# First-layer scores from one product of both mixing weights with x, in a two-layer f32 kernel

## The chip, the cores and the metric

The kernel runs on one core of a Trainium2 chip. The metric is the device time of one execution in microseconds (us). Three timed runs of the kernel before gave 1794.26, 1794.6 and 1798.48 us, a median of 1794.6. One more execution was profiled; its durations are the ones that the text uses.

The engines are called by their short names: PE is TensorE (PEld its weight loads), DVE is VectorE, ACT is ScalarE, POOL is GpSimd, SP is the engine that issues most DMAs.

## What is computed

Two layers over 32 batches. The first is a cross-attention of 128 channels by 512 positions per batch, the second a recurrent block (RWKV) that takes four batches as one group. Only the first layer matters here:

```python
def _L0_xattn_ref(x_c, x_s, Wn, bn, Wm, bm, Wl, bl, Wo, bo):
    Mn = _conv1x1(Wn, bn, _inorm(x_c))          # [128, 512] per batch
    Mm = _conv1x1(Wm, bm, _inorm(x_s))
    A = jax.nn.softmax(jnp.einsum('bct,bcs->bts', Mn, Mm), axis=-1)   # 512 x 512 per batch
    Ml = _conv1x1(Wl, bl, x_s)
    Mo = jnp.einsum('bcs,bts->bct', Ml, A)
    return _conv1x1(Wo, bo, Mo) + x_c
```

`_inorm` takes mean and variance of each channel over the 512 positions; `_conv1x1(W, b, x)` is W times x plus a bias per output channel. With x and y for the two normalised inputs, the score of token t against position s is

(Wn x_t + bn) . (Wm y_s + bm) = (Wm' Wn x_t + Wm' bn) . y_s + (Wn' bm . x_t + bn . bm),

where ' is the transpose. The last bracket does not depend on s: it is the same for all scores of token t. All arithmetic is f32.

## The kernel before

Everything that the engines execute in the main part is first recorded and then ordered. A call such as `K.tensor.matmul(...)` does not issue an instruction; it appends an operation with an estimated duration to a list (`Program.record`, `cost`). A list scheduler (`schedule`, `order_of`) simulates the five engines, gives out the buffers (8 PSUM banks, 44 work tiles of 128x512, 40 small tiles, 4 weight tiles of 1 MB) and fixes one order per engine; `pace` moves some DMAs. The rank of an operation is its place in the program, moved by the length of its chain and by a number of the table `SHIFTS` for its stage; the names with "+" apply to the last groups as well. `with K.bunch(ns)` makes several instructions one operation of the given duration. Since every recorded instruction is issued from the same helper, nearly all of them carry line 246 in the profile, and groups are told apart by tiles: `bank` is a PSUM bank, `t` a work tile, `small` a small tile, `wring` a big weight.

The first layer, `layer0(b)`, handles one batch: it loads x_c and x_s (256 KB each), takes statistics on DVE (`bn_stats`, `bn_aggr`), the reciprocal root on POOL, and normalises both inputs on DVE. Each normalised input goes through one product with its own 128x128 weight into a PSUM bank, from which ACT adds the bias: m_n and m_m. A third small set of products makes the values (four products of 128 columns with `wol`, the product of Wl and Wo). Then, for each of the four blocks `tb` of 128 tokens: one product of 128x512 scores, the negated maximum of each token's scores on DVE, exp on ACT with that maximum as bias and the sum as a second output, reciprocal and scaling on DVE. Sixteen transposes through PE and four products with the values finish the batch.

The first layer of a group is not run by itself. `ahead(place)` inserts the next group's batches into the second layer of the current one, and the scheduler uses them to fill PE while the recurrence works on DVE. Set-up stands outside the recorded part: the loads of four 128x128 weights and the biases on ACT's queue, and two products, `wol` and `bol` (lines 661 and 665).

In f32 each product is executed as two passes, so one matmul statement gives two matmul records and two weight loads.

Of the kernel before, what the change touches and what calls it, by code (L numbers as in the profile page):

```python
# [12 lines left out]
F32 = mybir.dt.float32  # L13
AF = mybir.ActivationFunctionType
ALU = mybir.AluOpType
# [3 lines left out]
P = 128  # L19
# [7 lines left out]
NC = E // P  # L27
# [33 lines left out]
SWITCH = 95  # L61
ROUNDS, TRACE, BLAME = 16, 20000, 0.001
SHIFTS = {
    "first0": -306, "first0+": -95, "first1": 2, "first1+": -122, "first2": -40,
    "first2+": -7, "first3": 24, "first3+": 203, "front": 7, "front+": 157, "gates": -67,
    "gates+": -1, "head": -121, "head+": 51, "levels0": -68, "levels0+": -71, "levels2": 20,
    "levels2+": -152, "mixes": 81, "mixes+": -41, "norm": 78, "norm+": -310,
    "outputs0": -277, "outputs0+": 238, "outputs2": -235, "outputs2+": -661,
    "recurrence0": -14, "recurrence0+": -48, "recurrence2+": -68, "rows": 85, "rows+": 306,
    "squares": -88, "squares+": 77, "values0": -56, "values0+": -63, "values2": 33,  # L70
    "values2+": 81,
}
REACH, PULL = 200, 0.003
WORDS, REFILL = 280, 3200
# [534 lines left out]
def xattn_then_rwkv(ctx: ExitStack, tc: tile.TileContext, a: dict, out: bass.AP):  # L609
    nc = tc.nc  # L610

    const = ctx.enter_context(tc.tile_pool(name="const", bufs=1))
    psum = ctx.enter_context(tc.tile_pool(name="psum", bufs=1, space=PSUM))

    def slots(tag, count, shape, space=const):
        return [space.tile(shape, F32, tag=f"{tag}{i}", name=f"{tag}{i}") for i in range(count)]

    banks = Pool(slots("bank", 8, [P, 512], psum))
# [10 lines left out]
    K = Program(nc, tc)  # L629

    def bank():
        return View(Tensor(banks, [P, 512]))

    def wt(shape=(P, 512)):
        return View(Tensor(work, list(shape)))
# [4 lines left out]
    def st_(*shape):  # L640
        return View(Tensor(small, [P, *shape]))


    ident = const.tile([P, P], F32, tag="ident", name="ident")
# [5 lines left out]
    w0 = {}  # L650
# [5 lines left out]
    bias = {n: bias4[:, i : i + 1] for i, n in enumerate(BIASES)}  # L656


    wol = const.tile([P, P], F32, tag="wol", name="wol")
    p0 = banks.tiles[7]  # L660
    nc.tensor.matmul(p0[:, 0:P], w0["Wl0"], w0["WoT0"], start=True, stop=True)
# [103 lines left out]
    def mean_rstd(stats, n):  # L765

        mv, rstd = st_(n, 2), st_(n)
        for i in range(n):
            K.vector.bn_aggr(mv[:, i, :], stats[:, i, :])
        K.vector.tensor_scalar(rstd, mv[:, :, 1], EPS, None, ALU.add)  # L770
        K.gpsimd.tensor_tensor(rstd, rstd, neg_half[:, 0:n], ALU.pow)
        return mv, rstd
# [10 lines left out]
    def layer0(b):  # L783
        K.stage = ("first", b, str(b % G))
        x_c, x_s = wt(), wt()
        K.held = begun.get(b - 2)
        K.sync.dma_start(x_c, a["x"][b])
        K.held = begun.get(b - 2)
        K.sync.dma_start(x_s, a["ctx_2048"][b])
        stats = st_(2, 6)  # L790
        K.vector.bn_stats(stats[:, 0, :], x_c)
        K.vector.bn_stats(stats[:, 1, :], x_s)
        mv, rstd = mean_rstd(stats, 2)
        m = []
        for i, (src, w, bi) in enumerate(((x_c, "WnT", "bn"), (x_s, "WmT", "bm"))):
            xn = wt()
            K.vector.tensor_scalar(
                xn, src, mv[:, i, 0:1], rstd[:, i : i + 1], ALU.subtract, ALU.mult
            )
            pm = bank()  # L800
            K.tensor.matmul(pm, w0[w], xn, start=True, stop=True)
            t = wt()
            K.scalar.activation(t, pm, AF.Identity, bias=bias[bi])
            m.append(t)
        m_n, m_m = m


        pv = bank()
        for sb in range(NC):
            K.tensor.matmul(  # L810
                pv[:, sb * P : (sb + 1) * P], x_s[:, sb * P : (sb + 1) * P], wol,
                start=True, stop=True,
            )
        vals = wt()
        K.scalar.copy(vals, pv)


        e = []
        for tb in range(NC):
            sc = bank()  # L820
            if tb == 0:
                begun[b] = K.ops[-1]
            K.tensor.matmul(sc, m_n[:, tb * P : (tb + 1) * P], m_m, start=True, stop=True)
            nmax, den = st_(1), st_(1)
            K.vector.tensor_reduce(nmax, sc, AX.X, ALU.max, negate=True)
            t = wt()
            K.scalar.activation(t, sc, AF.Exp, bias=nmax, accum_out=den)
            K.vector.reciprocal(den, den)
            K.vector.tensor_scalar(t, t, den, None, ALU.mult)
            e.append(t)  # L830
        po = bank()
        for sb in range(NC):
            pt = bank()
            for tb in range(NC):
                K.tensor.transpose(
                    pt[:, tb * P : (tb + 1) * P], e[tb][:, sb * P : (sb + 1) * P], ident
                )
            at = wt()
            K.scalar.copy(at, pt)
            K.tensor.matmul(  # L840
                po, vals[:, sb * P : (sb + 1) * P], at, start=(sb == 0), stop=(sb == NC - 1)
            )
        K.vector.scalar_tensor_tensor(x_c, po, bol, x_c, ALU.add, ALU.add)
        return x_c
# [256 lines left out]
    def layer1(g, xs):  # L1101
        following = []

        def ahead(place):

            stage = K.stage
            if g + 1 < NG:
                for i in (AHEAD if g + 2 < NG else AHEAD_LAST)[place]:
                    following.append(layer0((g + 1) * G + i))
            K.stage = stage  # L1110
# [190 lines left out]
    def feed_forward(g, xs, ws):  # L1301
# [42 lines left out]
        yield  # L1344

    xs = [layer0(0), layer0(1)]
    constants()
    xs += [layer0(2), layer0(3)]
    for g in range(NG):
        xs = layer1(g, xs)  # L1350
# [42 lines left out]
```

## Time and profile before

| | us |
|---|---|
| median of three runs | 1794.6 |
| profiled execution | 1798.06 |
| its span, first to last instruction | 1796.3 |
| PE busy | 1758.5 (98%) |
| PE weight loads busy | 888.7 (49%) |
| DVE busy | 1171.4 (65%) |
| ACT busy | 706.2 (39%) |
| POOL busy | 310.3 (17%) |
| PE, products of a normalised input with its weight (WnT and WmT, 128 records) | 67.5 |
| ACT, bias of these products (64 records) | 43.3 |

A group line of the profile reads: line, engine, operation, out<-in, array tile or shape, count, then busy time and mean duration in ns of one, then the idle time of the engine before them and what ended it. Matmul records overlap: a record of a 512-column pass has a mean of some 600 ns, though in a stream the passes follow each other at 429 ns. A timeline line gives the start in us, the duration of a merged group, and the group. The granted clock of PE is half of the full one before about 15 us and in a few short stretches, and full otherwise; its mean over the execution is 0.995.

### The profile page before, as it was taken

To read this page: it belongs to the slowest core of one execution; us is meant where nothing else is said; L and a number is where in the kernel's file an instruction comes from. 1 tells how busy PE (TensorE), PEld (TensorE's weight loads), DVE (VectorE), ACT (ScalarE), POOL (GpSimd) and SP (SyncE) were. 2 spreads that over 40 slices of the span, in tenths; PEclk is the share of its full clock that TensorE was granted. 3 is DMA by queue.
4 is the path that set the end of the run, shared out by engine and by line. 5 is a ranking of instruction groups with operands and counts; after the bars stand their busy time and mean duration, and the time that the engine had idled before them with its cause. 6 is when DMAs were issued, how large, how long until landed. Compare 5 with 4: busy or idle time off the path is not lost. (4 is left out here: it accounts for less than half of the span.)

```text
span 1796.3 us, 45435 instructions
## 1 busy us (share of the span) xinstructions
PE 1758.5 (98%) x20232; PEld 888.7 (49%) x20232; DVE 1171.4 (65%) x2301; ACT 706.2 (39%) x1230; POOL 310.3 (17%) x329
## 2 busy tenths in 40 slices
PE   8999999999999999999999999999999999899998
PEld 4435554456434554345543465445554345445543
DVE  9847784468935687456864578546784765786561
ACT  4524531356313563235632445324542245324321
POOL 2230014200150001600006000160010500320011
PEclk9999999999999999999999999999999999899999
DMA  6000131012120130101211022110221201001010
GB/s 206 21 0 3 37 119 62 9 41 73 59 70 1 41 108 26 69 2 53 96 47 47 2 58 90 53 41 2 63 85 59 73 25 49 3 0 61 15 36 35
DMA packets 61940, 87.23 MB, mean 49 GB/s; under 512 B 20336, under 2 KB 21488, under 8 KB 61744
## 3 DMA queue, kind: packets, MB, share of 16 engines
q1 hardware_dynamic: 61024, 84.06, 14.7%
q8 instruction: 158, 2.59, 0.6%
q14 instruction: 38, 0.31, 0.1%
q10 hardware_dynamic: 720, 0.26, 0.1%
HBM read 75.93 MB, written 8.39 MB: 47 GB/s over the span
## 5 line engine op out<-in xcount | busy, mean ns | idle before, releaser
L246 PE MATMUL bank<-t,wring 128*128 128x512 f32 x1024 | 469.0, 603 | 2.0 <-DVE t L246 2.0
L246 PE MATMUL bank<-wring,t 128*128 128x512 f32 x768 | 339.6, 595 | 0.7 <-DVE t L246 0.7
L246 PEld LDWEIGHTS bank<-t,wring 128*128 128x128 f32 x1024 | 187.2, 190 | 239.1 <-issue 205.4
L246 POOL TENSOR_TENSOR t<-t,t 128x512 f32<-128x512 f32 x192 | 239.4, 1285 | 349.3 <-DVE t L246 343.3
L246 DVE TENSOR_TENSOR t<-bank,t 128x512 f32<-128x512 f32 (+1 forms) x256 | 143.7, 585 | 211.4 <-PE bank L246 164.1
L246 POOL TENSOR_TENSOR small<-small,neg_half 128x1 f32<-128x1 f32 (+1 forms) x96 | 62.9, 661 | 1131.4 <-DVE small L246 1131.3
L246 PE MATMUL bank<-t,t 128*128 128x512 f32 x512 | 251.1, 607 | 2.1 <-ACT t L246 1.9
L246 PEld LDWEIGHTS bank<-wring,t 128*128 128x128 f32 x768 | 143.5, 190 | 185.7 <-issue 179.1
L246 ACT COPY t<-bank 128x512 f32<-128x512 f32 (+1 forms) x240 | 132.2, 589 | 218.3 <-PE bank L246 212.1
L246 ACT ACTIVATE t<-bank 128x512 f32<-128x512 f32 x120 | 71.4, 598 | 341.4 <-PE bank L246 341.3
L246 DVE SCALAR_TENSOR_TENSOR t<-bank,vec,t 128x512 f32<-128x512 f32 x192 | 131.4, 743 | 67.2 <-PE bank L246 67.2
L246 PEld LDWEIGHTS bank<-ident,t 128*128 128x128 f32 x900 | 104.5, 141 | 75.2 <-issue 43.6
L246 PE MATMUL bank<-ident,t 128*128 128x128 f32 x900 | 130.1, 276 | 4.6 <-ACT t L246 2.7
L246 ACT ACTIVATE wide<-rk,par 128x512 f32<-128x512 f32 x128 | 85.4, 715 | 122.4 <-DVE rk L246 122.4
L246 ACT ACTIVATE t<-bank,small 128x512 f32<-128x512 f32 x128 | 87.8, 690 | 106.2 <-DVE small L246 105.4
L246 PEld LDWEIGHTS bank<-t,t 128*128 128x128 f32 x512 | 87.0, 189 | 85.6 <-issue 56.3
L246 PEld LDWEIGHTS bank<-wide,rk 32*64 32x64 f32 x8192 | 95.6, 131 | 55.3 <-ACT wide L246 17.0
L246 PE MATMUL bank<-t,wv 128*128 128x512 f32 x256 | 122.6, 603 | 0.0
L246 DVE COPY_PREDICATED at<-level,bank 128x512 f32<-128x512 int32 x192 | 121.5, 704 | 0.0
L246 PE MATMUL bank<-wide,rk 32*64 32x64 f32 x8192 | 105.9, 233 | 8.2 <-issue 3.8
L246 DVE TENSOR_REDUCE small<-bank 128x1 f32<-128x512 f32 x128 | 85.9, 680 | 30.8 <-PE bank L246 30.4
L246 DVE SCALAR_TENSOR_TENSOR t<-t,vec,t 128x512 f32<-128x512 f32 x128 | 90.9, 755 | 0.1
(98 smaller groups left out, 1796.4 us busy)
## 6 DMA issues: line engine op xcount, KB each, us to landing
t<-in_ctx_dram SPq DMA_DIRECT2D x32, 256.0 KB, 3.2
t<-in_x_dram SPq DMA_DIRECT2D x32, 256.0 KB, 3.0
wring<-in_WgT_dram SPq DMA_DIRECT2D x8, 1024.0 KB, 5.2
wring<-in_WkT_dram SPq DMA_DIRECT2D x8, 1024.0 KB, 5.3
wring<-in_WrT_dram SPq DMA_DIRECT2D x8, 1024.0 KB, 5.2
wring<-in_WoT_dram SPq DMA_DIRECT2D x8, 1024.0 KB, 5.6
out_dram<-t SPq DMA_DIRECT2D x32, 256.0 KB, 2.0
wring<-in_WfkT_dram SPq DMA_DIRECT2D x7, 1024.0 KB, 5.2
```

The source lines that it names most:

```text
L246: done[op] = f(*[real(x) for x in args], **{k: real(x) for k, x in kw.items()})
```

## The change

Set-up gains a product of the two mixing weights. Since the weights arrive transposed, both are first transposed through PE and copied by DVE to `nat`; their product goes to `wq`. Three single-column products give Wm' bn, Wn' bm and bn . bm (the last broadcast to all 128 partitions), copied to `qwc` as qb, wb and cb.

In each batch the normalised x goes through one product with `wq`, and ACT adds qb: q. The normalised y is used as it is, so the second product and its bias go. The part common to a token's scores comes from four products of x_n's 128-token blocks with the single column wb, recorded as one operation of 480 ns, and DVE adds cb. For each token block, DVE adjusts the negated maximum by that common part (it subtracts it and adds it), between the maximum and the exp that uses it.

The table SHIFTS gets new numbers, so the scheduler's order is drawn again for all stages.

```diff
 SHIFTS = {
-    "first0": -306, "first0+": -95, "first1": 2, "first1+": -122, "first2": -40,
...
+    "first0": -289, "first0+": -139, "first1+": -80, "first2": -32, "first2+": 88,
...
+    nat = {}
+    for i, n in enumerate(("WnT", "WmT")):
+        nat[n] = const.tile([P, P], F32, tag=f"nat{i}", name=f"nat{i}")
+        pn = banks.tiles[4 + i]
+        nc.tensor.transpose(pn[:, 0:P], w0[n], ident)
+        nc.vector.tensor_copy(nat[n], pn[:, 0:P])
+    wq = const.tile([P, P], F32, tag="wq", name="wq")
+    pq = banks.tiles[3]
+    nc.tensor.matmul(pq[:, 0:P], nat["WnT"], nat["WmT"], start=True, stop=True)
+    nc.vector.tensor_copy(wq, pq[:, 0:P])
+    qwc = const.tile([P, 3], F32, tag="qwc", name="qwc")
+    bn_bc = const.tile([P, P], F32, tag="bn_bc", name="bn_bc")
+    nc.vector.tensor_copy(bn_bc, bias["bn"].to_broadcast([P, P]))
+    pw = banks.tiles[2]
+    for i, (left, right) in enumerate(
+        ((nat["WmT"], bias["bn"]), (nat["WnT"], bias["bm"]), (bn_bc, bias["bm"]))
+    ):
+        nc.tensor.matmul(pw[:, i : i + 1], left, right, start=True, stop=True)
+    nc.vector.tensor_copy(qwc, pw[:, 0:3])
+    qb, wb, cb = (qwc[:, i : i + 1] for i in range(3))
...
-        m = []
-        for i, (src, w, bi) in enumerate(((x_c, "WnT", "bn"), (x_s, "WmT", "bm"))):
-            xn = wt()
+        xn = []
+        for i, src in enumerate((x_c, x_s)):
+            xn.append(wt())
             K.vector.tensor_scalar(
-                xn, src, mv[:, i, 0:1], rstd[:, i : i + 1], ALU.subtract, ALU.mult
-            )
-            pm = bank()
-            K.tensor.matmul(pm, w0[w], xn, start=True, stop=True)
-            t = wt()
-            K.scalar.activation(t, pm, AF.Identity, bias=bias[bi])
-            m.append(t)
-        m_n, m_m = m
+                xn[i], src, mv[:, i, 0:1], rstd[:, i : i + 1], ALU.subtract, ALU.mult
+            )
+        x_n, y_n = xn
+        pm = bank()
+        K.tensor.matmul(pm, wq, x_n, start=True, stop=True)
+        q = wt()
+        K.scalar.activation(q, pm, AF.Identity, bias=qb)
+
+        pc = bank()
+        with K.bunch(480):
+            for tb in range(NC):
+                K.tensor.matmul(
+                    pc[:, tb : tb + 1], x_n[:, tb * P : (tb + 1) * P], wb, start=True, stop=True
+                )
+        same = st_(NC)
+        K.vector.tensor_scalar(same, pc[:, 0:NC], cb, None, ALU.add)
...
-            K.tensor.matmul(sc, m_n[:, tb * P : (tb + 1) * P], m_m, start=True, stop=True)
+            K.tensor.matmul(sc, q[:, tb * P : (tb + 1) * P], y_n, start=True, stop=True)
             nmax, den = st_(1), st_(1)
             K.vector.tensor_reduce(nmax, sc, AX.X, ALU.max, negate=True)
+
+            part = same[:, tb : tb + 1]
+            K.vector.scalar_tensor_tensor(nmax, nmax, part, part, ALU.subtract, ALU.add)
             t = wt()
             K.scalar.activation(t, sc, AF.Exp, bias=nmax, accum_out=den)
```

## The prediction

> **What bounds the kernel now.** I read the busy shares first, then the busy time by stretches, then the timeline around single TensorE instructions, and last the groups by form for prices.
>
> ```profile
> PE 1758.5 (98%) x20232; PEld 888.7 (49%) x20232; DVE 1171.4 (65%) x2301; ACT 706.2 (39%) x1230; POOL 310.3 (17%) x329
> ```
>
> ```profile
> 0.00:20.00 20.00, 12.20 (x39) 8.23 (x40) 15.89 (x41) 5.33 (x9) 10.08 (x44) 1.00 0.61 190
> 300.00:1500.00 1200.00, 1191.54 (x13779) 600.96 (x13776) 780.47 (x1541) 484.70 (x841) 213.22 (x201) 1.00 0.16 50
> 1500.00:1620.00 120.00, 110.00 (x1432) 55.52 (x1416) 89.64 (x159) 44.12 (x76) 28.91 (x26) 0.96 0.06 19
> ```
>
> The second fence has, after each stretch and its length, the busy time of PE, PEld, DVE, ACT and POOL, then granted clock, DMA share and GB/s. TensorE is the bound almost throughout: in the 1200 us of the middle it is idle for 8.5 us. It loses 7.8 us in the first 20 us and 10 us between 1500 and 1620. So what the change does to TensorE's own queue is paid in full, and what it does to DVE, ACT and POOL counts only where TensorE then has nothing to do.
>
> Two prices decide: a pass over 512 columns, and what a pass costs whose columns are few, so that only the weight load is left. These are timelines of TensorE and of its weight loads at four places, taken separately (start, duration of the merged group):
>
> ```profile
> 257.06 0.30 PEld L246 LDWEIGHTS bank<-t,t 128*128 128x128 f32 x2 [0.28 <-ACT t L246]
> 257.59 0.19 PEld L246 LDWEIGHTS bank<-t,t 128*128 128x128 f32 x1 [0.24 <-ACT t L246]
> 258.02 0.19 PEld L246 LDWEIGHTS bank<-t,t 128*128 128x128 f32 x1 [0.24 <-issue]
> ...
> 15.99 1.05 PE L246 MATMUL bank<-wol,t 128*128 128x128 f32 x8
> ...
> 140.50 0.42 PEld L246 LDWEIGHTS bank<-ident,t 128*128 128x128 f32 x4 [0.92 <-ACT t L246]
> ...
> 163.31 0.59 PE L246 MATMUL bank<-t,wv 128*128 128x512 f32 x1
> 163.84 0.76 PE L246 MATMUL bank<-vp,t 64*32 64x32 f32 x64
> ```
>
> Every f32 product is two passes, each with its own load. At 257 us TensorE had been idle. The first load starts at 257.06; the second ends 0.30 later and lasts 0.19, so it starts 0.11 after the first; the third starts 0.53 after the first and the fourth 0.43 after that. So a 512-column pass takes 0.43 (0.429 over a long stream), and nothing can follow a 128x128 f32 load on the load path before about 0.11. The eight 128-column passes at 15.99 agree: (1.05 - 0.275) / 7 = 0.111 each, 0.275 being the last one's own duration. The load of a transpose is cheaper: of four at 140.50 the first three steps take 0.42 - 0.14 = 0.28, of which two are the 0.109 of a streamed 128-column transpose, so the first load held the path for 0.06. Last, a 512-column pass followed by a product on small array tiles takes 163.84 - 163.31 = 0.53 in place of 0.43: changing the tile shape costs about 0.093.
>
> **The change part by part.**
>
> *TensorE, per batch (32 times).* One 512-column product goes: 2 x 0.429 = 0.858 us. Four single-column products come, eight passes, each with a fresh 128x128 load of x_n. A pass over one column has no streaming to speak of, so it costs what the load path needs. Ends: 0.061 (the transposed load) gives 0.49 a batch, a gain of 0.37 x 32 = 11.8 us; 0.190 (the whole duration of a load, nothing overlapped) gives 1.52, a loss of 0.66 x 32 = 21.2 us. I take 0.111, the row with the same load, type and shape: 0.89 a batch, +0.03 x 32 = **+1.0 us**. The only single-column row of this trace is at half clock:
>
> ```profile
> L665 PEld LDWEIGHTS bank<-bias,WoT 128*128 128x128 f32 x2 | 0.5, 333 | 0.0
> L665 PE MATMUL bank<-bias,WoT 128*128 128x1 f32 x2 | 0.4, 282 | 0.0
> ```
>
> Its two passes last 0.42 together, 0.21 each at half clock, about 0.11 at full: the same value.
>
> [...] A stream of single columns at full clock is in no run yet.
>
> *Changes of tile shape.* In the built order, TensorE's queue goes 427 times from one tile shape to another before, 413 times after: -14 x 0.093 = **-1.3 us**.
>
> *Start.* Before, DVE reaches the first batch's statistics at 8.94 and TensorE its first layer product at 12.56:
>
> ```profile
> 8.94 0.68 DVE L246 BATCH_NORM_STATS2 small<-t 128x6 f32<-128x512 f32 x1
> ...
> 12.56 2.08 PE L246 MATMUL bank<-t,WnT 128*128 128x512 f32 x2 [1.23 <-DVE t L246]
> ```
>
> In the built order five new copies stand ahead of those statistics in DVE's queue (bn_bc, two nat, wq, qwc), and the last waits for TensorE, where ahead of the three set-up singles stand one wol product, two transposes, four wol products and the product of the two weights: 14 passes. TensorE is at half clock there, 0.22 a pass (the 16 wol passes from 7.55 take 3.78). From 7.78 (bn_bc delays wol by a copy of 0.23) 14 x 0.22 = 3.1 and six single passes x 0.21 = 1.3 lead to 12.2; with the qwc copy and two casts (0.25) the statistics start near 12.7, 3.7 late, and the q product near 16.3. Two passes at half clock (0.85 each), eight single passes (0.22) and two wol products bring the first score to about 20.4, against 16.93. By then it has done one 512-column product and two wol products less and four singles more, 0.4 us. So up to 3.9 us; if the clock rises during this, less. I take **+3.0**, ends 1 and 5. DVE's adjustment of the first batch waits for its singles with the next batch's normalisation queued behind it; that lies inside these ends. On SP's queue the 1 MB load of wv moves behind one x and one ctx load, 256 KB each (3 us to landing); its first reader stood at 19.75, so it hides behind the scores. POOL's queue keeps its 330 rows.
>
> *DVE and ACT.* Each batch adds on DVE one 128x4 add and four 128x1 adjustments; the nearest row is the 128x1 tensor_scalar:
>
> ```profile
> L246 DVE TENSOR_SCALAR small<-small 128x1 f32<-128x1 f32 x64 | 9.1, 147 | 0.7
> L246 ACT ACTIVATE t<-bank,bias 128x512 f32<-128x512 f32 x64 | 43.3, 686 | 25.7 <-PE bank L246 25.2
> ```
>
> 160 x 0.15 = 24 us more on DVE (65% to 67%); the second row halves, 22 us less on ACT, worth nothing since ACT is at 39%. The new wait: exp waits for the adjustment and no longer for the maximum, 0.15 plus a hand-over on DVE, some 0.25, with reciprocals and scalings of other blocks behind it in DVE's queue and the transposes of that block behind exp. Cover: TensorE's other 98% of work. Ends: 0, and 128 x 0.25 = 32 us if each were waited for. TensorE's own waits for DVE:
>
> ```profile
> PE bank L246 <- DVE t L246: 8.2, 7, 2.0
> PE bank L246 <- DVE at L246: 2.1, 1, 2.1
> PE bank L246 <- DVE rk L246: 1.8, 1, 1.8
> ```
>
> About 12 us for 1171 us of DVE work, 1%. So 24 us more make **+0.3**.
>
> *Order.* The whole order is drawn again (new shifts; the two listings of TensorE's queue share few stretches). There is no price for it: what it can win or lose is TensorE's idle time between start and end, about 25 us, and the half-clock stretches (clock 0.80 from 93 to 110, 0.96 from 1500 to 1620), about 8. I take 0, ends -8 and +10.
>
> **Sum.** +1.0 - 1.3 + 3.0 + 0.3 = +3.0 us. The profiled execution took 1798.06 (span 1796.3 and 1.8 around it), 3.5 above the median of 1794.6; taken to the median: 1797.6.
>
> **The rivals.** (1) *Slower by waits for DVE.* The score chain grew by 0.25 us in 128 places, and the planner counts a batch's singles at 480 ns where I count 890, so TensorE's later work meets DVE and PSUM buffers in another phase than planned. For it: DVE is at 75% in 1500 to 1620, where TensorE already idles 10 us. Against: 1% in the whole. If a third of the 128 is waited for, +10.6: 1808. It decides from a tenth on (+3). (2) *Faster by cheap singles*: the load path takes 0.061 as for transposes: 1797.6 - 12.8 = 1784.8. For it: that row and the 480 ns. Against: the f32 rows. (3) *Faster by a better order*: half of what 1500 to 1620 loses (10 idle, about 5 by the clock) comes back: 1790. Against: nothing in this trace points to it. (4) *Loads without overlap*, 0.190 a pass: 1817.8; against it, the 0.111 row. That the change does not do what it says is excluded: the built order holds 32 products with wq and 128 with single columns.
>
> **How the numbers follow.** Mine 46% (1797.6, own range 1792 to 1804), (1) 30%, (2) 9%, (3) 13%, (4) 2%. The range leaves out most of (2) below and the far part of (1) with (4) above: 1787 to 1811. Some 0.3% (5.4 us, bounds 1789.2 and 1800.0) is what a measurement of this kernel tells from no change. Faster: nearly all of (2) and half of (3), 0.16. Slower: (1), (4) and a fifth of mine, 0.41. Within: the rest, 0.43.
>
> **What would show it.** Singles: 256 matmul records of 128x1 whose loads stand 0.11 apart, a batch's eight taking 0.89; loads 0.06 apart would be rival 2, 0.19 rival 4. Start: the first scores near 20 us and PE busy under 12.2 in the first 20. DVE: busy near 1195, PE's waits for DVE near 12; for rival 1 they, or the loads' waits for ACT and DVE, are 10 more. If PE's waits and the clock of 1500 to 1620 carry the difference, it was the order.

## The result and the profile after

The changed kernel takes 1793.09 us, median of 20 runs (1790.09 to 1795.3), against 1794.96 for the kernel before in 20 runs beside it (1790.83 to 1799.02). The ratio is 0.9988, 95% interval 0.9982 to 0.9995: 2.2 us less (0.9 to 3.2). That is inside the 0.3% that the prediction called "within", but it is a gain, where 3 us of loss were forecast.

The profiled execution took 1793.18 (span 1791.5), at the median. That of the kernel before took 1798.06 (span 1796.3), 3.1 above its 20-run median. So an account of the two traces has to explain 4.8 us of span, of which some 3 are that one execution's own.

The busy shares of the changed kernel:

```profile
PE 1759.7 (98%) x20434; PEld 903.8 (50%) x20434; DVE 1195.1 (67%) x2466; ACT 681.9 (38%) x1198; POOL 313.4 (17%) x329
```

DVE's 1195 us are as forecast. TensorE is as busy as before (1758.5), but its idle time, span less busy, fell from 37.8 to 31.8 us. Where, the busy time by stretches shows (columns as in the prediction: PE, PEld, DVE, ACT, POOL, granted clock, DMA share, GB/s; the 1.00 in the first row is no reading, since no clock is on record before 22.9 us and the passes there run at half clock, as shown below). The changed kernel:

```profile
0.00:20.00 20.00, 10.88 (x42) 9.49 (x43) 13.13 (x37) 3.14 (x4) 10.20 (x43) 1.00 0.40 129
20.00:1500.00 1480.00, 1474.08 (x16818) 756.99 (x16817) 1010.87 (x2123) 585.85 (x1043) 262.75 (x248) 1.00 0.16 52
93.00:110.00 17.00, 16.67 (x50) 6.33 (x49) 13.21 (x21) 0.87 (x1) 16.53 (x13) 1.00 0.00 0
300.00:1500.00 1200.00, 1195.77 (x14011) 611.43 (x14010) 797.68 (x1648) 469.78 (x823) 212.71 (x198) 1.00 0.16 50
1500.00:1620.00 120.00, 110.11 (x1280) 54.70 (x1279) 80.24 (x150) 40.40 (x69) 28.04 (x26) 0.94 0.07 23
```

The same view of the kernel before, the two stretches not shown yet:

```profile
20.00:1500.00 1480.00, 1465.14 (x16519) 739.49 (x16518) 981.47 (x1959) 605.62 (x1067) 258.98 (x247) 1.00 0.16 50
93.00:110.00 17.00, 15.23 (x31) 5.89 (x31) 9.21 (x13) 1.28 (x1) 14.50 (x12) 0.80 0.00 1
```

From 20 to 1500 us TensorE was idle for 14.86 us and is now idle for 5.92: 8.9 us less. And from 93 to 110 the mean clock was 0.80 and is now 1.00, worth 0.2 x 17 = 3.4 us. The timeline of TensorE there shows what went; first the kernel before, then the changed one:

```profile
92.80 1.98 PE L246 MATMUL bank<-t,wring 128*128 128x512 f32 x4
96.55 4.05 PE L246 MATMUL bank<-t,w2a 32*128 32x512 f32 x8 [1.77 <-DVE t L246]
100.53 6.55 PE L246 MATMUL bank<-t,wring 128*128 128x512 f32 x10
```

```profile
91.38 3.70 PE L246 MATMUL bank<-t,wring 128*128 128x512 f32 x8
95.01 1.14 PE L246 MATMUL bank<-t,w2a 32*128 32x512 f32 x8
96.08 2.84 PE L246 MATMUL bank<-t,wring 128*128 128x512 f32 x6
```

Before, TensorE waits 1.77 us for DVE, and then the eight `w2a` passes take 4.05 us where the changed kernel's take 1.14. Part of that is the clock, which is at half in the kernel before from 97.7 on:

```profile
97.70:104.60 6.90, 6.90 (x11) 2.84 (x10) 3.79 (x6) 0.00 (x0) 6.90 (x7) 0.51 0.01 2
```

After, the wait is not there, and neither is the drop. The wait and the drop together cost 1.8 + 3.4, about 5 us. The drop belongs to the old order and not to this one execution: the profiles of the four other kernels in that order (below) have one of 3.4 or 6.8 us that begins between 103 and 110 us (mean clock from 93 to 110: 0.90 in setup_only, 0.81 in adjust_only), each 2.7 to 4.4 us after the start of a wait of 1.4 to 1.8 us ahead of `w2a`; no kernel in the changed kernel's order has one there (1.00 from 93 to 110 in singles_twice, singles_six, no_singles_same_order, setup_on_act and setup_all_on_act). That the wait causes it is not shown: waits of 2.0 us at 1428 and 1.8 us at 1616 in the kernel before have no drop behind them (clock 1.00 from 1420 to 1432 and from 1608 to 1622).

The other stretches go the opposite way. At the start, the eight first scores end 4.6 us later than before with 0.4 us less work done by then, so TensorE loses about 5.0 us (next section but one). After 1500 us it is idle for 16.7 us in place of 15.2 up to the last instruction, and around 1540 it has half clock for 13.7 us in place of 10.2: 1.5 + 1.7, some 3.2 us more together. With the singles' +1.1 and the -1.3 forecast for the tile shapes: 5.0 - 12.3 + 3.2 + 1.1 - 1.3 = -4.3 against the -4.8 of the spans.

**The price of the singles.** Timelines of TensorE's weight loads and of its products around one batch's singles at full clock, and their groups over the whole kernel:

```profile
85.01 0.19 PEld L246 LDWEIGHTS bank<-qwc,t 128*128 128x128 f32 x1 [0.24 <-issue]
85.44 0.86 PEld L246 LDWEIGHTS bank<-qwc,t 128*128 128x128 f32 x7 [0.24 <-issue]
86.22 0.30 PEld L246 LDWEIGHTS bank<-t,t 128*128 128x128 f32 x2
```

```profile
85.44 0.95 PE L246 MATMUL bank<-qwc,t 128*128 128x1 f32 x8
86.25 1.10 PE L246 MATMUL bank<-t,t 128*128 128x512 f32 x2
```

```profile
L246 PEld LDWEIGHTS bank<-qwc,t 128*128 128x128 f32 x256 | 33.5, 196 | 12.8 <-issue 12.0 <-DVE t L246 0.8
L246 PE MATMUL bank<-qwc,t 128*128 128x1 f32 x256 | 30.9, 245 | 0.0
L246 DVE SCALAR_TENSOR_TENSOR small<-small,small 128x1 f32<-128x1 f32 x128 | 26.9, 225 | 0.4
L246 DVE TENSOR_SCALAR small<-bank,qwc 128x4 f32<-128x4 f32 x32 | 6.1, 203 | 21.7 <-PE bank L246 21.6
```

Loads overlap passes here: the first load of the next product starts at 86.22, and the record of the last single pass ends at 86.39 (85.44 + 0.95). The load of the batch's second single pass starts at 85.44; the loads of the next product's two passes start at 86.22 and, since the group of two lasts 0.30 and one load 0.19, at 86.33. From the second load of the singles to the second load of the next product are eight passes: 0.892 to 0.893 us, 0.1115 each, against the forecast 0.89. Over 32 batches that is 28.6 us, 1.1 more than the 27.5 of the products that went. The adjustment takes 225 ns in DVE's records, where 150 had been taken; from the end of a maximum (393.97 us) to the end of its adjustment (394.22) pass 0.25 us, the 0.25 of the prediction.

### The profile page after: what moved, and what is told of

Its sections match the earlier page's. It is cut to its first block, busy times and chain, and to the rows that moved or that the text cites. A ratio compares the mean times of both kernels' runs of the same rounds, so it can differ in the third digit from the quotient of the medians.

```text
span 1791.5 us, 45991 instructions
## 1 busy us (share of the span) xinstructions
PE 1759.7 (98%) x20434; PEld 903.8 (50%) x20434; DVE 1195.1 (67%) x2466; ACT 681.9 (38%) x1198; POOL 313.4 (17%) x329
## 4 chain that ended last, share of the span: by engine, by line
PE 89%; ACT 3%; DVE 3%; issue 3%; POOL 2%; DMA 0%; POOLq 0%; SPq 0%; ACTq 0%; DVEq 0%
PE bank L246 89%; POOL t L246 1%; DVE t L246 1%; ACT at L246 1%; DVE small L246 1%; ACT wide L246 1%; ACT t L246 0%; DMA t<-in_x_dram 0%; ACT L246 0%; DVE rk L246 0%; DVE at L627 0%; DVE vp L627 0%; POOLq L1423 0%; POOL small L246 0%; PE bank L677 0%
## 5 line engine op out<-in xcount | busy, mean ns | idle before, releaser
L246 PE MATMUL bank<-t,t 128*128 128x512 f32 x512 | 255.8, 609 | 0.7 <-ACT t L246 0.2
```

Source lines behind the costliest of these rows:

```text
L246: done[op] = f(*[real(x) for x in args], **{k: real(x) for k, x in kw.items()})
```

## The experiments

In all kernels marked "same order" the scheduler plans from one kernel's list, and only what is issued differs. For this, an operation got a field `emit`: if it is set, these calls are issued in place of the recorded ones.

```diff
-            for attr, method, args, kw in op.calls:
+            for attr, method, args, kw in op.calls if op.emit is None else op.emit:
```

All differences in us below are a ratio less one, times 1796, with its 95% interval in brackets. "Against the changed kernel" goes through the kernel before, which ran beside every kernel; the errors of both ratios are then in it, some 2 to 3 us (about 5 for singles_twice).

| run | median us | ratio to before (95%) | us |
|---|---|---|---|
| changed kernel | 1793.09 | 0.9988 (0.9982 to 0.9995) | -2.2 |
| new_math_old_order | 1823.32 | 1.0151 (1.0137 to 1.0164) | +27.1 |
| after_old_shifts | 1810.5 | 1.0078 (1.0065 to 1.0091) | +14.0 |
| before_new_shifts | 1799.11 | 1.0015 (1.0006 to 1.0024) | +2.7 |
| setup_only | 1800.86 | 1.0026 (1.0013 to 1.0039) | +4.7 |
| singles_twice | 1829.33 | 1.0206 (1.0181 to 1.0231) | +37.0 |
| singles_six | 1817.9 | 1.0116 (1.0102 to 1.013) | +20.8 |
| no_singles_same_order | 1768.19 | 0.9853 (0.9839 to 0.9866) | -26.4 |
| no_adjust | 1789.78 | 0.9977 (0.9967 to 0.9986) | -4.1 |
| adjust_only | 1814.36 | 1.0105 (1.009 to 1.0121) | +18.9 |
| old_order_no_adjust | 1799.87 | 1.0028 (1.0017 to 1.0039) | +5.0 |
| setup_on_act | 1790.89 | 0.9982 (0.9973 to 0.9991) | -3.2 |
| setup_all_on_act | 1788.16 | 0.9954 (0.9941 to 0.9966) | -8.3 |
| bunch_890 | 1813.34 | 1.01 (1.0084 to 1.0116) | +18.0 |
| no_common | 1803.68 | 1.0048 (1.0032 to 1.0063) | +8.6 |

The theory going in: the direct terms cost a few us and the order drawn again repays them. The rival: the terms are cheaper than worked out, and the order does nothing.

### Computation and order taken apart

**The new computation in the old order.** The product with WnT becomes the one with `wq`, the product with WmT becomes the four singles into the same bank, ACT copies y and adds cb, and the adjustment goes behind each maximum.

```diff
+            K.ops[-1].emit = [("tensor", "matmul", (pm, wq, x_n), go)] if i == 0 else [
+                ("tensor", "matmul", (pm[:, k : k + 1], x_n[:, k * P : (k + 1) * P], wb), go)
+                for k in range(NC)
+            ]
...
+            K.ops[-1].emit = K.ops[-1].calls + [(
+                "vector", "scalar_tensor_tensor", (nmax, nmax, part, part, ALU.subtract, ALU.add), {}
+            )]
```

> The new computation (product with wq, four single-column products, adjustment of the maximum, set-up) is issued in exactly the order of the kernel before: the planner plans the old operations, and only what is issued is replaced. ACT copies y instead of adding a bias, and adds cb. Theory 'order': the terms of the prediction hold (+1.1 us singles, +3.0 start, +0.3 DVE), and the gain that was measured came from the new order; so this is 3 to 6 us slower than before (about 1799). Rival 'the change itself gains' (one bias and one product less ahead of the scores): as fast as the changed kernel or faster, 2 us under before.

Measured: +27.1 us (24.6 to 29.5), far over the expectation. The stretch view and TensorE's waits (us in total, times, longest) of this kernel:

```profile
20.00:1500.00 1480.00, 1456.23 (x16044) 742.87 (x16043) 989.42 (x2052) 596.63 (x1074) 258.82 (x247) 1.00 0.16 51
```

```profile
PE bank L248 <- DVE t L248: 13.1, 22, 3.1
PE bank L248 <- ACT t L248: 10.8, 21, 1.8
```

TensorE is idle for 23.8 us from 20 to 1500, against 14.9 before and 5.9 in the changed kernel, and it waits for ACT's tiles in 21 places (4.7 us in 10 places before) and for DVE's in 22 (8.2 us in 7 places before). The transposes (`ident,t`, those behind exp among them) and the products of two work tiles (`t,t`) have 11.9 and 5.0 us of idle time ahead of them in this kernel, 4.6 and 2.1 in the kernel before. In the old order the computation is a clear loss.

**The change with the old table, and the old kernel with the new table.**

```diff
 SHIFTS = {
-    "first0": -289, "first0+": -139, "first1+": -80, "first2": -32, "first2+": 88,
+    "first0": -306, "first0+": -95, "first1": 2, "first1+": -122, "first2": -40,
...
```

> The changed kernel, planned with the old SHIFTS table. Theory 'order': the new table was worth what the new computation lost and more, so this is 3 to 12 us above the changed kernel (1796 to 1805). Rival 'the change itself gains': within 1.5 us of the changed kernel (1793).

> The kernel before, planned with the new SHIFTS table. Theory 'order': an order drawn again moves the time by several us either way, so this differs from before by 2 to 10 us; the sign is not forecast, since the table was made for another list of operations. Rival 'the change itself': the table is of no account, within 1.5 us of before.

Measured: +14.0 us (11.7 to 16.3) for the change with the old table, so the scheduler repairs about half of the 27 us by planning with the new list, and the table brings another 16, more than the 3 to 12 expected. The old kernel with the new table: +2.7 us (1.1 to 4.3). The table is no better in itself: it fits the new list and not the old one. The stretch view of the change with the old table:

```profile
20.00:1500.00 1480.00, 1463.29 (x16394) 747.88 (x16393) 1003.68 (x2103) 585.46 (x1034) 262.16 (x248) 1.00 0.16 51
```

Its idle time there is 16.7 us, 10.8 more than with the new table.

**The set-up alone.** The kernel before, in its own order, with the new set-up and nothing that uses it.

```diff
+    wq = const.tile([P, P], F32, tag="wq", name="wq")
+    pq = banks.tiles[3]
+    nc.tensor.matmul(pq[:, 0:P], nat["WnT"], nat["WmT"], start=True, stop=True)
+    nc.vector.tensor_copy(wq, pq[:, 0:P])
...
```

> The kernel before with the new set-up products and copies added and not used, old order otherwise. It measures the start by itself. Theory: DVE's first statistics move from 8.9 to about 12.4 us and the whole by +3.0 (1 to 5). Rival 'the start is hidden' (later work has slack that takes it up, or the clock rises earlier): under +0.7.

Measured: +4.7 us (2.3 to 7.0). Timelines of DVE and of TensorE in this kernel:

```profile
11.99 1.28 DVE L246 BATCH_NORM_STATS2 small<-t 128x6 f32<-128x512 f32 x2
```

```profile
20.90 3.41 PE L246 MATMUL bank<-t,t 128*128 128x512 f32 x7
```

The first statistics wait until 11.99 (8.94 before), the first scores until 20.90 (16.93 before). So 'the start is hidden' is out.

### The price of a single column

**The singles issued twice**, in the changed kernel's order.

```diff
                     pc[:, tb : tb + 1], x_n[:, tb * P : (tb + 1) * P], wb, start=True, stop=True
                 )
+        K.ops[-1].emit = K.ops[-1].calls * 2
```

> The changed kernel with every batch's four single-column products issued twice, order otherwise the same. It measures their price. Theory: 8 more passes of 0.112 us a batch, 32 x 0.893 = +28.6 us over the changed kernel (about 1822). Rival 'cheap singles' (0.061 a pass): +15.6. Rival 'hidden beside other work': under +5.

Measured: 39 us over the changed kernel (35 to 44 by this kernel's own ratio), 10 more than the expectation. Its timeline of TensorE and its stretches around one place:

```profile
426.32 5.04 PE L248 MATMUL bank<-qwc,t 128*128 128x1 f32 x32
```

```profile
426.00:431.00 5.00, 5.00 (x33) 4.76 (x32) 3.72 (x7) 2.15 (x4) 0.00 (x0) 0.73 0.00 0
431.00:436.00 5.00, 5.00 (x23) 3.19 (x30) 0.92 (x3) 0.59 (x1) 0.00 (x0) 0.59 0.00 0
```

TensorE is busy without a gap, yet its clock falls. Two batches' singles stand together here, 32 passes, at full clock 32 x 0.1115 = 3.6 us. The clock falls while they run, 2.0 us after the first of them here (426.3 to 428.3). The trace has five such places (428, 654, 879, 1104 and 1329 us), each with 6.8 us at half clock, so 3.4 lost. Then 28.6 + 5 x 3.4 = 45.6, which is the rise of PE's busy time (1759.7 to 1805.3) in the profiled execution; the other runs of this kernel are faster by 9 to 13 us. So in the profiled execution the doubled passes cost what was forecast, and the surplus is the clock.

**Six singles a batch in place of four.**

```diff
+        K.ops[-1].emit = K.ops[-1].calls + K.ops[-1].calls[0:2]
```

> The changed kernel with six single-column products a batch in place of four (two are issued again), order the same. Twice the singles had cost about 37 us and showed five stretches of 6.8 us at half clock, each after two batches' singles had stood together (32 passes, 3.6 us). [...] Rival 'a pass costs more than 0.112': +18, half of the 37.

Measured: 23 us over the changed kernel, 8.6 over the 14.3 that the added passes come to at their price (32 x 4 x 0.1116). There are four stretches with 3.4 us at half clock (424, 646, 1090 and 1312 us), each behind a pair of 24 passes, 24 x 0.1115 = 2.7 us: 14.3 + 4 x 1.7 = 21. The fifth such pair (866 us) has none behind it. One of the four in the stretch view of this kernel:

```profile
424.00:428.00 4.00, 4.00 (x78) 2.50 (x78) 1.43 (x4) 0.59 (x1) 0.00 (x0) 0.57 0.00 0
```

In the changed kernel the pairs have 16 passes, 16 x 0.1115 = 1.8 us (at 415, 633, 852, 1071 and 1289 us), and no drop follows them: the clock is on record as full from 22.9 to 1531.6 us. TensorE is 100% busy in the rows where its clock falls (5.00 of 5.00 us at 0.73, 4.00 of 4.00 at 0.57), so the busy time of the profile does not tell of the drops; what brings them on is not shown.

**No singles**, in the changed kernel's order, with the singles, cb's addition and the adjustments left out (a number common to all scores of a token drops out of the softmax).

```diff
+        K.ops[-1].emit = []
         same = st_(NC)
         K.vector.tensor_scalar(same, pc[:, 0:NC], cb, None, ALU.add)
+        K.ops[-1].emit = []
...
             K.vector.scalar_tensor_tensor(nmax, nmax, part, part, ALU.subtract, ALU.add)
+            K.ops[-1].emit = []
```

> The changed kernel without the part common to a token's scores: single-column products, the addition of cb and the adjustment are left out, the rest stands in the same order. The common part does not change the softmax. Theory: -28.6 us from the singles and -0.3 from DVE against the changed kernel, if the work behind them can move up (about 1764). Rival 'other engines set the pace behind them': half of it or less, 1779 or more.

Measured: 24 us under the changed kernel, where 28.9 were expected. PE's busy time fell by 30.2 us (to 1729.5), its idle time rose by 2.8 (to 34.6, with a span of 1764.1). So nearly all of the singles' time is on the path: what leaves TensorE's queue leaves the span, less a small part that turns into waits.

### The adjustment on DVE

**Without it, in the changed kernel's order; and it alone, with zeros, in the kernel before and its order; and the new computation in the old order without it.**

```diff
             K.vector.scalar_tensor_tensor(nmax, nmax, part, part, ALU.subtract, ALU.add)
+            K.ops[-1].emit = []
```

```diff
             K.vector.tensor_reduce(nmax, sc, AX.X, ALU.max, negate=True)
+            part = zeros[:, tb : tb + 1]
+            K.ops[-1].emit = K.ops[-1].calls + [(
+                "vector", "scalar_tensor_tensor", (nmax, nmax, part, part, ALU.subtract, ALU.add), {}
+            )]
```

> The changed kernel without the 128 adjustments of the maximum on DVE (the common part is computed and then left out), order the same. Theory: the new wait ahead of exp is covered by TensorE's other work, -0.3 us, within 1 us of the changed kernel. Rival 'slower by waits for DVE': a third of 128 x 0.3 us is waited for, 8 us or more faster than the changed kernel.

> The kernel before, old computation and old order; only the adjustment of the maximum is added (128 times on DVE, with zeros for the common part). The new computation in the old order had cost 26.7 us. Theory 'unplanned wait': most of it is this operation of 0.23 us between the maximum and exp, for which the old order leaves no room; +14 to +22 us over before. Rival 'the singles and ACT's copy are at the wrong places': under +5, and the next run stays slow.

> The new computation in the old order as before, with the 128 adjustments left out (the common part is computed and not used). Theory 'unplanned wait': what is left is the singles (+1.1) and the start (+4.7 as measured), with a little for ACT's copy: +5 to +9 over before. Rival 'wrong places': +20 or more.

Measured: the adjustment is worth 2.0 us in the changed kernel, about the error of that comparison. In the old order it costs 18.9 us (16.2 to 21.7) by itself, and taking it out of the new computation in the old order brings +27.1 down to +5.0. So 19 to 22 us of the 27 are these 128 instructions of 0.225 us, 29 us of DVE time: in that order two thirds or more of it is waited for. TensorE's waits in the kernel before with the adjustment alone, then one line of the kernel before as it was:

```profile
PE bank L248 <- ACT t L248: 11.5, 22, 1.8
PE bank L248 <- DVE t L248: 11.0, 23, 1.7
```

```profile
PE bank L246 <- ACT t L246: 4.7, 10, 1.8
```

Waits for ACT's tiles went from 10 to 22 places (4.7 to 11.5 us), those for DVE's from 7 to 23 (8.2 to 11.0). Seen from TensorE the chain is maximum, adjustment, exp, scaling, transposes. The two kernels issue the same 20232 passes in the same order, so their starts can be set side by side: of the 16.0 us between the two spans, 11.9 are lost ahead of transposes (`ident,t`), 5.0 ahead of `t,t`, and the rest about cancels. Only 7.6 of the 16.0 show as idle time: a pass's record is longer than its place in the stream (a transpose's 0.28 us against 0.11), so a short delay leaves no gap.

### The set-up moved to another engine

**Four of the set-up's copies on ACT and the one of bn_bc on POOL; then all five on ACT.** Both have the whole computation and the changed kernel's order.

```diff
-        nc.vector.tensor_copy(nat[n], pn[:, 0:P])
+        nc.scalar.copy(nat[n], pn[:, 0:P])
...
-    nc.vector.tensor_copy(bn_bc, bias["bn"].to_broadcast([P, P]))
+    nc.gpsimd.tensor_copy(bn_bc, bias["bn"].to_broadcast([P, P]))
```

> The changed kernel with four of the five set-up copies on ACT and the broadcast of bn on POOL, order otherwise the same. Theory: DVE's first statistics go back from 12.4 to about 9 us, and the changed kernel's start loses 3 us less: 1790. Rival 'the start is hidden': within 0.7 us of the changed kernel.

> The changed kernel with all five set-up copies on ACT; with bn's broadcast on POOL the masks made there came later and DVE's first statistics still began at 11.7. Theory: statistics near 9, first score about 3 us earlier than 20.4, and 3 to 4 us off the changed kernel (about 1789.5). Rival 'the start is hidden': within 1 us of it.

Measured: the first is within the error of the changed kernel (1.1 us less than it) and did not do what it was for: the first statistics still stand at 11.66 and the first scores at 20.27. DVE's timeline in this kernel names POOL:

```profile
11.57 0.26 DVE L246 CAST level<-small 128x32 int32<-128x32 f32 x1 [2.02 <-POOL small L246]
11.66 1.28 DVE L246 BATCH_NORM_STATS2 small<-t 128x6 f32<-128x512 f32 x2
```

The copy stands ahead of POOL's other set-up work, and DVE waits 2.02 us for a small tile of that ahead of the statistics. With all five on ACT, 8.3 us less than the kernel before (6.1 to 10.6), 6.1 less than the changed kernel. Its timelines of DVE and of TensorE:

```profile
8.94 1.27 DVE L246 BATCH_NORM_STATS2 small<-t 128x6 f32<-128x512 f32 x2
```

```profile
17.52 4.88 PE L246 MATMUL bank<-t,t 128*128 128x512 f32 x8
```

The statistics are back at 8.94, the time of the kernel before, and the first scores come 2.9 us earlier than in the changed kernel. Set beside the changed kernel pass by pass (the order is the same), TensorE is 2.9 us ahead at 20 us and 3.2 at 1600: so the trace gives the start about 3 of the 6.1 us, as expected, and the rest, within the errors, is not explained. The eight first scores still take 4.88 us, so the late rise of the clock stays. This is the fastest kernel of the study with the whole computation.

### The planner told other numbers

**The bunch of singles planned with their measured time.**

```diff
-        with K.bunch(480):
+        with K.bunch(893):
```

> The changed kernel, planned with 893 ns for a batch's singles in place of 480, the new table kept. Theory 'an order is a draw and the table was fitted to one list': another list of durations gives another order, to which the table was not fitted; 3 to 15 us over the changed kernel. Rival 'a right price makes a better plan': up to 5 us under it.

Measured: +18.0 us, 20 over the changed kernel, more than the 3 to 15 expected. A more truthful duration with the same table gives a worse order.

**The common part left out, and planned so** (set-up copies on ACT, new table). The softmax does not depend on it.

```diff
-        pc = bank()
-        with K.bunch(480):
...
-            K.vector.scalar_tensor_tensor(nmax, nmax, part, part, ALU.subtract, ALU.add)
```

> The changed kernel without the part common to a token's scores (single-column products, addition of cb, adjustments; the softmax does not depend on it), planned without it, new table, and the set-up copies on ACT. Theory: singles -28.6, adjustments -2, start -6, together -36 (about 1757), with an order term of unknown sign up to 10. Rival 'the cover is gone': no better than the 1768 of the fixed order without the common part.

Measured: +8.6 us, 11 over the changed kernel, where 36 under it were expected, and 35 us more than the kernel with the same singles left out in a fixed order (-26.4), although its set-up is the better one. Its stretches:

```profile
300.00:1500.00 1200.00, 1185.44 (x13818) 592.07 (x13817) 774.65 (x1532) 467.23 (x818) 205.04 (x195) 1.00 0.16 50
1500.00:1620.00 120.00, 107.29 (x1253) 53.48 (x1252) 72.96 (x133) 35.43 (x64) 28.17 (x26) 0.91 0.10 35
```

TensorE is idle for 14.6 us in the middle (4.2 in the changed kernel) and 12.7 from 1500 to 1620 (9.9), there with the clock at 0.91. Less work in an order that fits worse takes longer than more work in one that fits.

## Why the prediction was wrong

**Singles, +1.0: right.** The loads stand 0.1115 us apart, a batch takes 0.893 us, the term is +1.1. Rival 2 (0.061) and rival 4 (0.190) are out by the row, and the doubled and the six singles confirm the price once the clock is taken off.

**Tile shapes, -1.3:** not tested by itself. Counted in the traces by the rows and columns of a pass, the shape changes 456 times before and 449 after, 7 fewer and not 14, which at the prediction's price would be -0.7.

**Start, +3.0 with ends 1 and 5: right in mechanism, small in size.** The first scores were forecast for 20.4 and came at 20.45. The timelines of DVE and of TensorE in the changed kernel, then one line of TensorE's in the kernel before:

```profile
11.07 0.29 DVE L669 COPY wq<-bank 128x128 f32<-128x128 f32 x1 [1.06 <-PE bank L668]
12.14 0.16 DVE L678 COPY qwc<-bank 128x3 f32<-128x3 f32 x1 [0.78 <-PE bank L677]
12.38 1.28 DVE L246 BATCH_NORM_STATS2 small<-t 128x6 f32<-128x512 f32 x2
```

```profile
16.02 2.08 PE L246 MATMUL bank<-t,wq 128*128 128x512 f32 x2 [2.43 <-DVE t L246]
17.89 1.71 PE L246 MATMUL bank<-qwc,t 128*128 128x1 f32 x8
19.46 1.20 PE L246 MATMUL bank<-wol,t 128*128 128x128 f32 x4
20.45 4.82 PE L246 MATMUL bank<-t,t 128*128 128x512 f32 x8
```

```profile
16.93 3.70 PE L246 MATMUL bank<-t,t 128*128 128x512 f32 x8
```

DVE waits for TensorE ahead of the copies of wq and qwc, and the statistics follow at 12.38 (forecast 12.7). But eight score passes take 4.82 us in place of 3.70: the clock is still low when they begin (full clock is on record from 22.9 us on, from 15.8 in the kernel before). The estimate moved the work by 3.5 us but let the clock be up by the first scores, as it had been before. The term measured +4.7 with the set-up alone and about +5.0 in the traces, at the end of 5; taking the copies off DVE gave about 3 of it back. (PE's busy time in the first 20 us is 10.88, as forecast under the 12.2 named as the sign.)

**DVE and ACT, +0.3 with ends 0 and 32: right on this order, for a reason that does not hold in general.** Measured 2.0 here and 18.9 in the old order. The estimate scaled TensorE's waits for DVE by the share of DVE time added (2% more work, 2% more waits). That rule fails: what counts is whether the place of each adjustment in the chain has slack, and the old order had none. Rival 1 is the right mechanism for a change put into a fixed order; the new order hides it. TensorE's waits for DVE in the changed kernel, forecast at 12 us:

```profile
PE bank L246 <- ACT wide L246: 5.8, 2, 3.0
PE bank L246 <- DVE t L246: 5.3, 5, 2.4
PE bank L246 <- DVE rk L246: 1.4, 1, 1.4
```

With the 0.6 of the set-up the waits for DVE are 7.3, fewer than before in spite of 24 us more of work; the weight loads' waits for DVE's `t` fell too (70.0 to 53.0 us), those for ACT's rose by 4.3 (66.3 to 70.6). So the 10 us more that would have shown rival 1 are not there.

**Order, "I take 0, ends -8 and +10": this is the step that failed.** The direct terms as measured are +1.1 (singles), -1.3 (shapes, as forecast), +4.7 to +5.0 (start) and +2.0 (adjustment): +6.5 to +6.8. The result is -2.2, so the order brought about -9, where 0 was put; with errors of 2 to 3 us that is at the end of -8 or beyond it. The trace has it as 8.9 us less idle from 20 to 1500 and 3.4 us less lost to the clock, with some 3.2 given back after 1500. (The adjustment is counted here at its price in the new order. Against the same computation in the old order, the new order is worth 29 us: 27.1 + 2.2.) That it is the order, and not a smaller price of the parts, is shown by the same computation in the old order, +27.1, and with the old table, +14.0. The end of -8 had no more behind it than the 0. The prediction had read 25 us of idle time and 8 us of half clock as what an order could win, and then set the end at a quarter of that with no row behind the quarter. On the other side +10 was as narrow: planned without a table made for it, the list took 16 us (old table) and 20 us (893 in place of 480) longer than in the fitting order, and the shorter list without the common part 35.

That 1793.1 still lies inside the prediction's own range of 1792 to 1804 is luck: direct terms about 3.5 us too low and an order term 9 us too high partly cancel.

Rival 3 (a better order, 1790) is the one that came true in kind, in another place than it named: 1500 to 1620 won nothing, the middle did. The prediction said that nothing in the trace pointed to it; the wait of 1.77 us at 95 us with the dropped clock behind it was there to be read, and so were 14.9 us of idle time before 1500.

What stays open: which numbers of the table make this order fit. The runs show that the pair of list and table is good and that each half with the other's partner is not; why is not shown.

## What to carry to other kernels

A price taken from the row with the same load, type and shape held to 1% (0.1115 us a pass), even for a form that the trace did not have. Where a scheduler redraws the order, the redraw is a term of the sum of the same size as the change or more (here about -9 with a fitted table, and 16 to 35 us worse than that without one), so bound it by that and not by zero; and to learn what a change itself costs, issue it in the old order first. An added instruction on an engine with a third of its time free can still cost two thirds of its duration if it stands in a chain that comes just in time (here 18.9 of 29 us, with DVE busy for 65%).

## What the runs showed of the hardware

TensorE's clock fell to half at stretches of single-column products although its records show it 100% busy: behind 24 passes in a row (2.7 us) for 3.4 us in four places of five (singles_six), during 32 (2.0 to 2.3 us after the first) for 6.8 us in five of five (singles_twice), and not with 16 (1.8 us) in five of five (the changed kernel). What brings the clock down there is not shown; a transpose or a small-tile product in place of the singles was not tried. In the kernel before, a drop of 6.8 us begins 1.2 us after the end of an idle gap of 1.8 us (96.6 to 97.7), while gaps of 2.0 and 1.8 us elsewhere in the same trace have none behind them: the length of a gap alone does not decide.
